# Two attention blocks on one core: a third tile for transposed blocks, and smaller work moved between the engines

## The chip, the core and the metric

The kernel runs on one core of a Trainium2 chip. The metric is the time of one execution on the device, in microseconds, as the median of several runs. The profile is of one further execution, taken by the hardware profiler; its rows carry the line numbers of the kernel before.

In what follows PE is the TensorE, DVE the VectorE, ACT the ScalarE and POOL the GpSimd engine; SP is the engine that here only issues transfers. Each engine works through its own instructions in order.

## The reference

Four images of 32 x 32 positions and 768 channels go through two attention layers. Each layer adds its result to its input:

```python
x = x + _L0_conv_ref(_gn(x), ...)      # 32 groups, no affine part
x = x + _L1_conv_ref(_gn(x), ...)
# in a layer, for each of 12 heads of 64 channels, S = 1024 positions:
q, k, v = ...                          # qkv = x @ Wqkv (second layer: + bias)
rel_h = jnp.einsum('bhwc,hkc->bhwk', r_q, Rh)
rel_w = jnp.einsum('bhwc,wkc->bhwk', r_q, Rw)
bias = rel_h[..., :, None] + rel_w[..., None, :]
attn = jax.nn.softmax(scale * q @ k.T + bias, axis=-1)
out = (attn @ v) @ Wproj + bproj
```

The second layer scales q once more before the position terms. Everything is float32.

## The kernel before

The two layers of four images make eight "images" in a row (`im` 0 to 7). The twelve heads of an image make six pairs (`pair` 0 to 5), so there are 48 pairs `g` in all. A pair has eight units `n`, each of 128 query positions for both heads. The main loop runs over (g, n); it writes out the order of every engine by hand (`tc.manual_schedule`), and overlaps the units like this. In the step of unit n the program emits

- what was queued for this step in the lists `early` and `later` (things put into `later` run two steps on, into `early` one step on),
- `biases` (L434, POOL) for unit n + 2, which forms the position bias of 128 x 1024 from the rows in `rel`,
- `scores` for unit n + 1: eight matmuls (L448), the addition of the bias with a running minimum (L457, DVE) and the exponential with its sum (L461, ACT),
- the reads back of transposed blocks, from the lists `behind` and `behind2` (L496, SP),
- `turn` for unit n (L485, DVE): 32 x 32 transposes into a tile `tb`; after every second unit, a quarter, the tile of each head is written to device memory (`td`, L488, SP) and later read back turned (`pt`),
- `divide` for unit n + 1: the reciprocal (L468, DVE) and the division of both heads' rows (L471, POOL),
- a share of the next pair's projections and of an output projection (`take(todo, share)`, PE), with their sums on DVE (L238, L240, L378, L379, L599, L601),
- after unit 6, `weigh` for quarters 0 and 1 (L514, PE, reads `pt` and v), and in unit 2 of the next pair for quarters 2 and 3.

Step 0 of the loop thus holds the scores of unit 1. Tiles come from pools; a tile whose pool has no free buffer makes its first writer wait for the last reader of the buffer's earlier tenant. `tb` has two buffers, one for each head. PSUM gives two tiles to scores (`ps_s`) and two to everything else (`ps_m`).

Position terms: `positions` multiplies q by a table (L396, PE), copies the result to a tile `t` (L401, ACT) and writes it to device memory (`tdr`, L403, issued by ACT). `diagonals` then reads it back along diagonals as `rel`, 16 transfers for each pair (L422, SP). They are issued in unit 4, ahead of quarter 1's `pt`.

Queries and keys: except in a plain pair (pair 0, and pair 1 of image 0) the projections use sums of inputs and of weights. `sum_weights` combines the weights of pair g + 2 in units 6 and 7 of pair g (L316 on ACT, L319, L321, L322 on DVE, L320, L323, L324 on POOL). `sum_input` combines the next image's columns in pair 5, one column in each of units 0 to 5 (L333 on ACT, L334 to L341 on DVE) and six halves in units 6 and 7 (L345).

Image boundary: in pair 4 the next image is loaded (L112), then normalised by `apply` in units 6 and 7 (L223, POOL except in image 0). Its statistics are gathered before. In images 0 to 2, columns of the next image pass through a tile `tmp` for that purpose, in units 5 and 7 of pairs 0 to 2.

Output: `project_out` (L590) reads the attention tiles and an output weight `wo`; the residual `res`, a tile of half an image row, is fetched ahead by `fetch` (L549, L569, SP), added to (L599, L601) and stored (L606). A `fetch` for the coming parts is queued in `later` behind each second part.

## Time and profile before

| what | value |
|---|---|
| median of three runs | 4094.45 us (4075.72, 4094.45, 4100.07) |
| the profiled execution | 4075.33 us, span of its instructions 4073.3 us |
| mean granted clock of PE | 0.947 |
| busy PE, DVE, POOL, ACT | 3568.1, 2951.5, 2893.8, 1177.7 us |
| moved by the DMA engines | 1089.25 MB, mean 267 GB/s |
| issues of td, pt, rel | 384, 384, 768 |

How to read its rows. A row of the windows view has the window, its length, then the busy time of PE, PE's weight loads (PEld), DVE, ACT and POOL, each with the number of instructions, and last the granted clock, the DMA engines' busy share and GB/s. A row of a timeline has the start and length in us, the engine, the line, the operation, the tile written and the tiles read, and the number of instructions merged; in brackets stands the idle time of the engine before it and what ended that. "SPq" is SP's queue of issues: its length is the time of issuing, not of the transfer. The trace counts two PE matmuls for each one that the program names (3072 for the 1536 of L448).

### The profile page before, as it was taken

Reading aid. Unit: us, or ns where it says so; the run is one execution under the profiler, and the core shown is the slowest. Engines: PE = TensorE matmul, PEld = TensorE weight load, DVE = VectorE, ACT = ScalarE, POOL = GpSimd, SP = SyncE. Lnnn points to the kernel's source line nnn. Section 1 sums busy time; section 2 is a strip of 40 time slices with the busy share of each in tenths; the row PEclk is TensorE's granted clock in tenths of the full one; section 3 lists DMA queues with packets and bytes.
Section 4 is the critical chain, followed back from the end, with each engine's and each line's share of the span. In section 5 each row is a group of like instructions: output and inputs, shape, how many; then the busy total and the mean of one; then the engine's idle time right before and its main releaser. Section 6 shows DMA issues by size and latency. Waiting matters only on the chain.

```text
span 4073.3 us, 55032 instructions
## 1 busy us (share of the span) xinstructions
PE 3568.1 (88%) x20652; PEld 1936.1 (48%) x20652; DVE 2951.5 (72%) x4197; ACT 1177.7 (29%) x1918; POOL 2893.8 (71%) x1771
## 2 busy tenths in 40 slices
PE   6989789897898978999789897899978999789999
PEld 3555355453454534545345453544535455344554
DVE  5967687776877768777687776867767677677776
ACT  2323232232232323323232232322323233222331
POOL 3877776777666777776776777777777776777774
PEclk9999899998999989999899998999989999899999
DMA  4778678786687876878678786788867788678878
GB/s 135 253 282 289 239 255 285 286 301 247 242 281 281 294 250 245 281 282 289 236 260 278 279 305 237 242 298 285 305 227 251 281 291 289 225 262 284 293 255 295
DMA packets 635659, 1089.25 MB, mean 267 GB/s; under 512 B 248320, under 2 KB 311296, under 8 KB 586240
## 3 DMA queue, kind: packets, MB, share of 16 engines
q1 hardware_dynamic: 579808, 1033.01, 71.8%
q10 hardware_dynamic: 55584, 52.72, 3.8%
q8 instruction: 162, 2.65, 0.3%
q14 instruction: 105, 0.86, 0.1%
HBM read 585.31 MB, written 500.27 MB: 267 GB/s over the span
## 4 chain that ended last, share of the span: by engine, by line
PE 51%; DVE 19%; DMA 16%; POOL 7%; issue 4%; SPq 2%; ACT 0%; DVEq 0%; ACTq 0%
PE pj L262 17%; DMA td<-tb 12%; PE av L514 11%; PE s L448 10%; PE o L590 6%; PE pv L364 5%; DVE tb L485 5%; POOL x L223 4%; DVE sc L457 3%; DMA pt<-td 2%; PE tp L396 2%; SPq L422 2%; DVE x L334 2%; POOL sc L434 1%; DVE x L345 1%
## 5 line engine op out<-in xcount | busy, mean ns | idle before, releaser
L471 POOL TENSOR_SCALAR sc<-sc,sm 128x1024 f32<-128x1024 f32 x768 | 916.2, 1204 | 1083.3 <-DVE sm L468 1076.5
L434 POOL TENSOR_TENSOR sc<-rel 128x1024 f32<-128x1024 f32 x768 | 1563.5, 2105 | 37.5 <-DMA rel<-tdr 37.5
L461 ACT ACTIVATE sc<-sc,sm 128x1024 f32<-128x1024 f32 x768 | 879.4, 1146 | 2274.0 <-DVE sm L457 2273.5
L485 DVE STREAM_TRANSPOSE tb<-sc 128x1024 f32<-128x1024 f32 x768 | 917.8, 1225 | 381.3 <-DMA td<-tb 378.0
L457 DVE CUSTOM_DVE_ANT_0 sc<-s,sc 128x1024 f32<-128x1024 f32 x768 | 909.6, 1221 | 263.8 <-PE s L448 177.3
L262 PE MATMUL pj<-x,w 64*128 64x512 f32 x4140 | 950.8, 601 | 81.0 <-POOL x L223 44.3
L514 PE MATMUL av<-pt,v 128*64 128x256 f32 x6144 | 763.7, 401 | 195.8 <-DMA pt<-td 110.6
L448 PE MATMUL s<-k,q 64*128 64x512 f32 x3072 | 767.4, 604 | 32.1 <-DVE sm L457 32.0
L590 PE MATMUL o<-attn,wo 128*128 128x512 f32 x1080 | 555.2, 668 | 189.4 <-DVE res L599 103.0
L514 PEld LDWEIGHTS av<-pt,v 128*64 128x64 f32 x6144 | 463.8, 144 | 525.5 <-DMA pt<-td 134.8
L262 PEld LDWEIGHTS pj<-x,w 64*128 64x128 f32 x4140 | 410.4, 190 | 589.6 <-issue 450.6
L364 PE MATMUL pv<-wv,x 64*128 64x256 f32 x4608 | 515.1, 376 | 0.4 <-DVE k L238 0.4
L364 PEld LDWEIGHTS pv<-wv,x 64*128 64x128 f32 x4608 | 448.0, 187 | 91.6 <-issue 40.9
L448 PEld LDWEIGHTS s<-k,q 64*128 64x128 f32 x3072 | 295.6, 190 | 349.9 <-issue 278.0
L590 PEld LDWEIGHTS o<-attn,wo 128*128 128x128 f32 x1080 | 218.1, 210 | 510.3 <-issue 271.2
L401 ACT COPY t<-tp 128x1024 f32<-128x1024 f32 x96 | 97.1, 1011 | 306.8 <-PE tp L396 265.1
L223 POOL TENSOR_SCALAR x<-x,nrm 128x512 f32<-128x512 f32 x84 | 176.6, 2115 | 0.0
L238 DVE TENSOR_TENSOR k<-pj,k 128x512 f32<-128x512 f32 x173 | 117.7, 689 | 63.0 <-PE pj L262 46.3
L461 ACT ACTIVATION_READ_ACCUMULATOR sc<-sc,sm 128x1 f32 x768 | 143.2, 186 | 0.0
L599 DVE SCALAR_TENSOR_TENSOR res<-o,bo,res 128x512 f32<-128x512 f32 x88 | 64.4, 745 | 91.0 <-PE o L590 90.7
L396 PEld LDWEIGHTS tp<-tab,q 64*128 64x128 f32 x1536 | 98.0, 188 | 45.1 <-issue 42.4
L601 DVE TENSOR_TENSOR res<-o,res 128x512 f32<-128x512 f32 x92 | 62.0, 683 | 70.1 <-PE o L590 69.4
(57 smaller groups left out, 1607.9 us busy)
## 6 DMA issues: line engine op xcount, KB each, us to landing
td<-tb SPq DMA_DIRECT2D x384, 1024.0 KB, 6.0
pt<-td SPq DMA_DIRECT2D x382, 1024.0 KB, 7.6
tdr<-t ACTq DMA_DIRECT2D x96, 512.0 KB, 6.6
w<-in_wqk SPq DMA_DIRECT2D x96, 384.0 KB, 6.6
rel<-tdr SPq DMA_DIRECT2D x760, 32.0 KB, 2.2
x<-in_x SPq DMA_DIRECT2D x84, 256.0 KB, 6.4
part<-res SPq DMA_DIRECT2D x84, 256.0 KB, 3.1
res<-part SPq DMA_DIRECT2D x84, 256.0 KB, 8.4
```

Of the source, the lines that this page charges most:

```text
L223: (nc.gpsimd if im else nc.vector).tensor_scalar(x, x, nrm[:, c, 0:1], nrm[:, c, 1:2], ALU.subtract, ALU.mult)
L262: nc.tensor.matmul(t[:, a, :], lhsT=w[rows, c, :], rhs=x[c][rows, :], start=(c == 0), stop=(c == len(x) - 1),)
L364: nc.tensor.matmul(t[:, a, k, :], lhsT=xs[i // 2 * NC + c][rows, at * P : (at + 1) * P], rhs=w[rows, c, :], start=(c == 0), stop=(c == NC ...
L396: nc.tensor.matmul(ps[:, h, j, :], lhsT=q[rows, at * P : (at + 1) * P], rhs=tabs[l][rows, :], start=True, stop=True,)
L434: nc.gpsimd.tensor_tensor(sc.rearrange("p (a k) (u l) -> p a l (k u)", a=4, l=8), rel[:, h, 0, n, :].unsqueeze(1).unsqueeze(2).to_broadcas ...
L448: nc.tensor.matmul(ps[h][:, cols], lhsT=q[rows, n * P : (n + 1) * P], rhs=k[rows, cols], start=True, stop=True,)
L457: nc.vector.tensor_tensor_reduce(out=sc, in0=ps[h], in1=sc, scale=-scale, scalar=BIG, op0=ALU.add, op1=ALU.min, accum_out=st[:, 0, h : h + 1],
L461: nc.scalar.activation(sc, sc, AF.Exp, bias=st[:, 0, h : h + 1], scale=-1.0, accum_out=st[:, 1, h : h + 1],)
L471: nc.gpsimd.tensor_scalar(sc, sc, st[:, 2, h : h + 1], 1.0, ALU.mult, ALU.mult)
L485: nc.vector.transpose(tb[:, :, j, :], sc_of[g, n, h])
L514: nc.tensor.matmul(av[rows, at * 2 * P : (at + 1) * 2 * P], lhsT=v_of[g][:, k, rows], rhs=pt_of[g, quarter, h][:, :, k, :], start=(k == 0) ...
L590: nc.tensor.matmul(t, lhsT=wo_of[im, o, c], rhs=attn_of[im * NP + c][:, cols], start=(c == c0), stop=(c == c1 - 1),)
```

## The change

- The pool of transposed tiles `tb` gets three buffers.
- Bias rows: `rel` becomes two tiles of four units each, with three buffers in all; `diagonals` issues 32 transfers of 16 KB instead of 16 of 32 KB.
- The pool `tmp` goes. Position copies and the columns for the statistics use the `res` tiles (four buffers, half the size), so a position copy becomes two, each with its own transfer. The statistics' columns are loaded in unit 1 of every pair (image 0: units 1 and 4 of pairs 0 to 2).
- `fetch` for a pair's four output parts runs in unit 5.
- The attention tile of a pair becomes two halves, eleven buffers instead of six whole ones.
- The query sums read PSUM and write the query in order, and read the key tile in steps, where they wrote in steps.
- Weights: the first sum moves from DVE to POOL; the two sums into `w4` become ACT copies of POOL's difference.
- Divisions: head 0 on POOL, head 1 on ACT.
- `apply` runs on DVE, spread over units 2, 4, 6 and 7.
- `sum_input` is spread over four steps for a column: ACT copy, POOL difference, DVE sum (with an ACT copy for the first three), DVE difference.

The core of the diff:

```diff
     xpool = ctx.enter_context(tc.tile_pool(name="x", bufs=1))
-    apool = ctx.enter_context(tc.tile_pool(name="attn", bufs=6))
+    apool = ctx.enter_context(tc.tile_pool(name="attn", bufs=11))
     qkpool = ctx.enter_context(tc.tile_pool(name="qk", bufs=2))
...
     scpool = ctx.enter_context(tc.tile_pool(name="sc", bufs=6))
-    tmppool = ctx.enter_context(tc.tile_pool(name="tmp", bufs=1))
-    tbpool = ctx.enter_context(tc.tile_pool(name="tb", bufs=2))
+    tbpool = ctx.enter_context(tc.tile_pool(name="tb", bufs=3))
     ptpool = ctx.enter_context(tc.tile_pool(name="pt", bufs=2))
-    relpool = ctx.enter_context(tc.tile_pool(name="rel", bufs=2))
+    relpool = ctx.enter_context(tc.tile_pool(name="rel", bufs=3))
     iopool = ctx.enter_context(tc.tile_pool(name="io", bufs=4))
...
         x, y = x_of[im - 1], y_of[im - 1]
-        x_of[im] = y[NC:] + x[:NC] + y[:3]
+        x_of[im] = spare(im - 1) + y[:3]
         y_of[im] = y[3:NC] + x[NC:]
+    def spare(im):
+        return y_of[im][NC:] + x_of[im][:NC]
     def load_x(im, c, i, to=None):
...
             x = x_of[im][i * NC + c]
-            (nc.gpsimd if im else nc.vector).tensor_scalar(
+            nc.vector.tensor_scalar(
                 x, x, nrm[:, c, 0:1], nrm[:, c, 1:2], ALU.subtract, ALU.mult
...
-        by = lambda x: x.rearrange("p (m a) -> p a m", a=4)
-        t = [by(t[:, a, :]) for a in range(2)]
-        q = [by(qk_of[g, 0][:, i * HALF : (i + 1) * HALF]) for i in range(2)]
+        q = [
+            qk_of[g, 0][:, i * HALF : (i + 1) * HALF].rearrange("p (m a) -> p m a", a=4)
+            for i in range(2)
+        ]
         k = qk_of[g, 1].rearrange("p (a m) -> p a m", a=4)
         k = [k[:, :, i * P : (i + 1) * P] for i in range(2)]
+        u = [t[:, a, :].rearrange("p (m a) -> p m a", a=4) for a in range(2)]
+        t = [x.rearrange("p m a -> p a m") for x in u]
         bias = [None, None]
...
             nc.scalar.copy(k[0], t[0])
-            add(q[0], t[1], k[0], bias[0])
+            add(q[0], u[1], k[0].rearrange("p a m -> p m a"), bias[0])
         elif unit == 1:
...
             add(k[1], t[0], k[0])
-            add(q[1], t[1], k[1], bias[0])
+            add(q[1], u[1], k[1].rearrange("p a m -> p m a"), bias[0])
         else:
...
         def second():
-            nc.vector.tensor_tensor(w3[TOP], w3[TOP], w[1][TOP], ALU.add)
+            nc.gpsimd.tensor_tensor(w3[TOP], w3[TOP], w[1][TOP], ALU.add)
             nc.gpsimd.tensor_tensor(w3[LOW], w3[TOP], w[0][TOP], ALU.subtract)
-            nc.vector.tensor_tensor(w4[TOP], w3[TOP, :3], w[0][TOP, :3], ALU.subtract)
-            nc.vector.tensor_tensor(w4[LOW], w3[TOP, 3:], w[0][TOP, 3:], ALU.subtract)
+            nc.scalar.copy(w4[TOP], w3[LOW, :3])
+            nc.scalar.copy(w4[LOW], w3[LOW, 3:])
             nc.gpsimd.tensor_tensor(w3[LOW], w[0][LOW], w3[LOW], ALU.subtract)
...
         xs, ys = x_of[im], y_of[im]
-        if n < NC:
-            a, b, y, z = xs[n], xs[NC + n], ys[n], ys[NC + n % 3]
+        def of(c):
+            return (xs[c], xs[NC + c], ys[c], ys[NC + c % 3]) if 0 <= c < NC else 4 * [None]
+        a, b, y, z = of(n)
+        if a is not None:
             nc.scalar.copy(y[LOW], b[TOP])
-            nc.vector.tensor_tensor(y[TOP], b[LOW], y[LOW], ALU.subtract)
-            if n < 3:
-                nc.vector.tensor_tensor(z[TOP], y[TOP], a[TOP], ALU.add)
-                nc.vector.tensor_tensor(y[LOW], y[TOP], a[TOP], ALU.add)
-                nc.vector.tensor_tensor(y[LOW], y[LOW], a[LOW], ALU.subtract)
-            else:
-                nc.vector.tensor_tensor(z[LOW], y[TOP], a[TOP], ALU.add)
-                nc.vector.tensor_tensor(y[LOW], z[LOW], a[LOW], ALU.subtract)
-            return
-        for c in range(3 * (n - NC), 3 * (n - NC) + 3):
-            a, b = xs[c], xs[NC + c]
-            (nc.gpsimd if c < 3 else nc.vector).tensor_tensor(b[TOP], b[TOP], a[TOP], ALU.subtract)
+        a, b, y, z = of(n - 1)
+        if a is not None:
+            nc.gpsimd.tensor_tensor(y[TOP], b[LOW], y[LOW], ALU.subtract)
+        a, b, y, z = of(n - 2)
+        if a is not None:
+            half = TOP if n - 2 < 3 else LOW
+            nc.vector.tensor_tensor(z[half], y[TOP], a[TOP], ALU.add)
+            if n - 2 < 3:
+                nc.scalar.copy(y[LOW], z[TOP])
+        a, b, y, z = of(n - 3)
+        if a is not None:
+            nc.vector.tensor_tensor(y[LOW], (y if n - 3 < 3 else z)[LOW], a[LOW], ALU.subtract)
+        for c in range(3 * n - 18, 3 * n - 15) if n in (6, 7) else ():
+            a, b, y, z = of(c)
+            (nc.gpsimd if c in (0, 3, 4) else nc.vector).tensor_tensor(
+                b[TOP], b[TOP], a[TOP], ALU.subtract
+            )
...
                 )
-        t = tmppool.tile([P, 4, 2, P], FP, tag="tmp", name=f"t_{g}_{i}")
-        nc.scalar.copy(t, ps.rearrange("p h j r -> p j h r"))
         td = t_of[g]
-        nc.scalar.dma_start(
-            out=td[i * HALF : (i + 1) * HALF, :].rearrange("(j p) r -> p j r", p=P),
-            in_=t.rearrange("p j h r -> p j (h r)"),
-        )
+        for k in range(2):
+            if g + 1 < NPAIR:
+                t = iopool.tile([P, 2, 2, P], FP, tag="res", name=f"t_{g}_{i}_{k}")
+            else:
+                t = spare(g // NP)[4 + 2 * i + k].rearrange("p (j h r) -> p j h r", j=2, h=2)
+            nc.scalar.copy(t, ps[:, :, 2 * k : 2 * k + 2, :].rearrange("p h j r -> p j h r"))
+            at = (2 * i + k) * 2 * P
+            nc.scalar.dma_start(
+                out=td[at : at + 2 * P, :].rearrange("(j p) r -> p j r", p=P),
+                in_=t.rearrange("p j h r -> p j (h r)"),
+            )
         if i == 1:
...
         td = t_of[g]
-        for h in range(2):
-            for ax in range(2):
-                for y in range(4):
+        rel_of[g] = []
+        for half in range(2):
+            rel = relpool.tile([P, 2, 2, NT // 2, HW], FP, tag="rel", name=f"rel_{g}_{half}")
+            rel_of[g].append(rel)
+            for h in range(2):
+                for ax in range(2):
+                    for y in range(4):
-                    at = HW * y * 2 * P + h * P + HW - 1 + 2 * HW * ax - (y if ax == 0 else 0)
-                    src = bass.AP(
-                        td.tensor, td.offset + at,
-                        [[2 * P - ax, HW], [P * 2 * P - (4 if ax == 0 else 0), NT], [1, HW]],
-                    )
-                    (nc.scalar if h and not g else nc.sync).dma_start(out=rel_of[g][32 * y : 32 * y + 32, h, ax, :, :], in_=src)
+                        step = P * 2 * P - (4 if ax == 0 else 0)
+                        at = HW * y * 2 * P + h * P + HW - 1 + 2 * HW * ax - (y if ax == 0 else 0)
+                        src = bass.AP(
+                            td.tensor, td.offset + at + half * (NT // 2) * step,
+                            [[2 * P - ax, HW], [step, NT // 2], [1, HW]],
+                        )
+                        (nc.scalar if h and not g else nc.sync).dma_start(
+                            out=rel[32 * y : 32 * y + 32, h, ax, :, :], in_=src
+                        )
...
             sc = sc_of[g, n, h].rearrange("p k j -> p (k j)")
-            nc.gpsimd.tensor_scalar(sc, sc, st[:, 2, h : h + 1], 1.0, ALU.mult, ALU.mult)
+            if h == 0:
+                nc.gpsimd.tensor_scalar(sc, sc, st[:, 2, h : h + 1], 1.0, ALU.mult, ALU.mult)
+            else:
+                nc.scalar.activation(sc, sc, AF.Copy, scale=st[:, 2, h : h + 1])
...
-        if quarters[0] == 0:
-            attn_of[g] = apool.tile([P, S], FP, tag="attn", name=f"attn_{g}")
+        half, first = divmod(quarters[0], 2)
+        if first == 0:
+            attn_of[g, half] = apool.tile([P, HALF], FP, tag="attn", name=f"attn_{g}_{half}")
         n = len(quarters)
...
             nc.tensor.matmul(
-                t, lhsT=wo_of[im, o, c], rhs=attn_of[im * NP + c][:, cols],
+                t, lhsT=wo_of[im, o, c], rhs=attn_of[im * NP + c, i],
                 start=(c == c0), stop=(c == c1 - 1),
...
                 fetch(place[im, p, o, i] + 4)
-            else:
-                later.append(lambda: fetch(place[im, p, o, i] + 4))
         yield True
...
         run(later)
-        fetch(3)
         biases(0, 0)
...
             early, later = later, early
-            if im + 1 < B and pair < 3 and n in (5, 7):
-                c = 2 * pair + n // 7
-                passing = tmppool.tile([P, S], FP, tag="tmp", name=f"x_{im + 1}_{c}")
+            upto = 4 * (pair % 3) + 3
+            if n == 5 and (im, pair) >= (0, 3):
+                fetch(place[((im, 0) if pair >= 3 else (im - 1, 1)) + divmod(upto, 2)])
+            ask = [divmod(g + 3, NP)] if n == 1 else []
+            if im == 0 and pair < 3:
+                ask = [(0, 2 * pair + n // 4)] if n in (1, 4) else []
+            for im2, c in ask if im < B else ():
                 for i in range(2):
-                    x = passing[:, i * HALF : (i + 1) * HALF]
-                    load_x(im + 1, c, i, x)
-                    later.append(lambda c=c, i=i, x=x: stats(im + 1, c, i, x))
+                    if im2 + 1 < B:
+                        x = iopool.tile([P, HALF], FP, tag="res", name=f"x_{im2 + 1}_{c}_{i}")
+                        load_x(im2 + 1, c, i, x)
+                        later.append(lambda im=im2 + 1, c=c, i=i, x=x: stats(im, c, i, x))
             if at + 2 < len(units):
...
                 divide(*units[at + 1])
-            if pair == 4 and n in (6, 7) and not end:
-                for c in range(4) if n == 6 else range(4, NX):
+            if pair == 4 and not end:
+                for c in {2: (0, 1), 4: (2, 3), 6: (4, 5, 6), 7: range(7, NX)}.get(n, ()):
                     apply(c % NC, c // NC)
...
                 sum_input(im + 1, n)
-            elif g == 0:
-                sum_input(0, n)
+            elif g == 0 or pair == 0 and n == 0:
+                sum_input(im, n if g == 0 else NT)
+            elif g == 1 and n == 0:
+                sum_input(0, NT)
             take(todo, share)
```

`spare(im)` names the nine input tiles that are free after the image's pair 4 (`y_of[im][NC:] + x_of[im][:NC]`). The places where a tile's new half is indexed, in `biases`, in the rest of `weigh`, and where `spare` takes the place of the same expression, are left out.

More of the change, by code (lines that the diff above doesn't have):

```diff
@@ L279, in project_in @@
             if which == 0:
-                to = qk_of[g, 0][:, i * HALF : (i + 1) * HALF].rearrange("p (m a) -> p m a", a=4)
-                t = [x.rearrange("p a m -> p m a") for x in t]
+                to, t = q[i], u
             if images[im][0] == 0:
@@ L389, in positions @@
             t_of[g] = dram2.tile([S, 2 * P], FP, tag="tdr", name=f"tdr_{g}")
-            rel_of[g] = relpool.tile([P, 2, 2, NT, HW], FP, tag="rel", name=f"rel_{g}")
         ps = ps_m.tile([P, 2, 4, P], FP, tag="m", name=f"tp_{g}_{i}")
@@ L411, in diagonals @@
         td = t_of[g]
-        for h in range(2):
-            for ax in range(2):
-                for y in range(4):
-                    at = HW * y * 2 * P + h * P + HW - 1 + 2 * HW * ax - (y if ax == 0 else 0)
-                    src = bass.AP(
-                        td.tensor, td.offset + at,
-                        [[2 * P - ax, HW], [P * 2 * P - (4 if ax == 0 else 0), NT], [1, HW]],
-                    )
-                    (nc.scalar if h and not g else nc.sync).dma_start(out=rel_of[g][32 * y : 32 * y + 32, h, ax, :, :], in_=src)
+        rel_of[g] = []
[14 more added lines that the diff above has]
+                        )
     sc_of, st_of, tb_of, pt_of, attn_of = {}, {}, {}, {}, {}
     def biases(g, n):
-        rel = rel_of[g]
+        rel, m = rel_of[g][n // 4], n % 4
         for h in range(2):
@@ L435, in biases @@
                 sc.rearrange("p (a k) (u l) -> p a l (k u)", a=4, l=8),
-                rel[:, h, 0, n, :].unsqueeze(1).unsqueeze(2).to_broadcast(shape),
-                rel[:, h, 1, n, :].rearrange("p (l a) -> p a l", a=4).unsqueeze(3).to_broadcast(shape),
+                rel[:, h, 0, m, :].unsqueeze(1).unsqueeze(2).to_broadcast(shape),
+                rel[:, h, 1, m, :].rearrange("p (l a) -> p a l", a=4).unsqueeze(3).to_broadcast(shape),
                 ALU.add,
@@ L517, in weigh @@
                     )
-        at = quarters[0] * 2 * P
-        to = attn_of[g][:, at : at + n * 2 * P].rearrange("p (q n r i) -> p q r n i", q=n, n=2, r=4)
+        at = first * 2 * P
+        to = attn_of[g, half][:, at : at + n * 2 * P].rearrange("p (q n r i) -> p q r n i", q=n, n=2, r=4)
         av = av.rearrange("p (q r n i) -> p q r n i", q=n, n=2, r=4)
@@ L565, in fetch @@
             else:
-                res = (y_of[im][NC:] + x_of[im][:NC])[2 * o + i - 4]
+                res = spare(im)[2 * o + i - 4]
             res_of[im, p, o, i] = res
```

## The prediction

> **What bounds the kernel now.** I read the page's totals and chain first, then the stretch of each pair of heads, then SP's and DVE's timelines in an ordinary pair.
>
> ```profile
> PE 3568.1 (88%) x20652; PEld 1936.1 (48%) x20652; DVE 2951.5 (72%) x4197; ACT 1177.7 (29%) x1918; POOL 2893.8 (71%) x1771
> ...
> PE pj L262 17%; DMA td<-tb 12%; PE av L514 11%; PE s L448 10%; PE o L590 6%; PE pv L364 5%; DVE tb L485 5%; POOL x L223 4%; DVE sc L457 3%; DMA pt<-td 2%; PE tp L396 2%; SPq L422 2%; DVE x L334 2%; POOL sc L434 1%; DVE x L345 1%
> ```
>
> TensorE carries half the chain; the rest is the trip of the transposed blocks through memory (td), some DVE, and POOL's normalisation (L223). Two rows of the windows view, a boundary pair (pair 5) and an ordinary one:
>
> ```profile
> 2477.90:2577.50 99.60, 79.59 (x441) 41.37 (x441) 77.43 (x94) 29.85 (x49) 79.90 (x45) 0.91 0.63 222
> 2662.70:2740.70 78.00, 71.99 (x427) 39.69 (x426) 54.01 (x81) 23.98 (x40) 56.52 (x36) 0.96 0.82 289
> ```
>
> The boundary pair is 21.6 us longer, with POOL busy 79.9 us. To see where, I cut each pair into eight stretches, from the start of L457 of one unit to that of the next, averaged over images 1 to 6. Pairs 0 to 5 take 87.5, 79.2, 79.6, 77.8, 82.9, 98.7 us. In pairs 1 to 4, stretches 1 to 6 (about 48 us) have PE busy throughout; the idle time lies in stretch 0 (17.3, 17.3, 16.8, 16.5 us, PE busy some 13) and stretch 7 (14.3, 14.5, 12.8, 16.4). Where no weights are combined before it, in pair 5, stretch 0 takes 12.4 us with PE full. In pair 5 stretches 1 and 2 take 22.0 and 16.7 us instead of some 7 and 8: POOL runs twelve L223 of 2.1 us there, and PE waits for x. Pair 0 opens with 26.1 us.
>
> SP's timeline in the ordinary pair 25, from unit 3 on, then PE's and DVE's:
>
> ```profile
> 2210.28 1.46 SPq L488 DMA_DIRECT2D td<-tb  x2
> 2212.14 9.91 SPq L422 DMA_DIRECT2D rel<-tdr  x16
> 2222.17 1.66 SPq L126 DMA_DIRECT2D w<-in_wqk  x1
> 2223.87 0.99 SPq L496 DMA_DIRECT2D pt<-td  x2
> 2224.95 1.31 SPq L488 DMA_DIRECT2D td<-tb  x2
> ```
>
> ```profile
> 2227.17 4.10 PE L514 MATMUL av<-pt,v 128*64 128x256 f32 x34
> 2233.33 3.67 PE L514 MATMUL av<-pt,v 128*64 128x256 f32 x30 [2.06 <-DMA pt<-td]
> ...
> 2250.87 5.26 PE L590 MATMUL o<-attn,wo 128*128 128x512 f32 x6 [4.04 <-DVE res L601]
> ```
>
> ```profile
> 2235.88 1.25 DVE L485 STREAM_TRANSPOSE tb<-sc 128x1024 f32<-128x1024 f32 x1 [6.13 <-DMA td<-tb]
> 2238.47 1.25 DVE L485 STREAM_TRANSPOSE tb<-sc 128x1024 f32<-128x1024 f32 x1 [1.35 <-DMA td<-tb]
> ...
> 2246.39 0.92 DVE L319 TENSOR_TENSOR w<-w,w 64x768 f32<-64x768 f32 x1
> 2247.35 1.35 DVE L321 TENSOR_TENSOR w<-w,w 64x384 f32<-64x384 f32 x1
> 2248.72 1.38 DVE L322 TENSOR_TENSOR w<-w,w 64x384 f32<-64x384 f32 x1
> 2250.12 0.69 DVE L601 TENSOR_TENSOR res<-o,res 128x512 f32<-128x512 f32 x1
> ```
>
> SP issues without a pause from 2210 to 2226. The block that PE wants in unit 6 (pt, quarter 1) is asked for at 2223.87, right behind sixteen rel transfers; both halves are there at 2233.3, and PE has waited 2.06 us. That is stretch 7. Then three weight sums hold L601, which PE needs: 4.04 us idle, and the next six matmuls take 5.26 us (877 each, against 444 in the group of 18 before): the clock fell. That is stretch 0.
>
> **The change, part by part.**
>
> *Bias rows in half tiles.* `diagonals` issues 32 transfers of 16 KB for 16 of 32 KB, all on SP ahead of quarter 1's pt. The price of one issue is the open number. Thirteen rel issues from 2215.62 take 6.43 us, 0.495 each; ten x loads of 256 KB at the start take 4.65 us, 0.465 each. Eight times the bytes costs no more, so I take the issue as fixed: 16 x 0.495 = 7.9 us more per pair. The bounds are 0 (price follows size) and 7.9; rel issues with a gap before them take 0.30, which would make 32 x 0.345 less 16 x 0.495, 3.1. Nothing covers it: PE already waits for this pt. Its later half lands on average 5.8 us after the start of stretch 7 (pairs 0 to 3), 8.3 in pair 4. In pair 4, where PE waits longest and restarts at half clock, stretch 7 is that landing plus 8.1 us. So after: 5.8 + 7.9 + 8.1 = 21.8 us in pairs 0 to 3, 24.3 in pair 4.
>
> [...]
>
> *Three tb tiles.* Two heads share the tag. With three, unit 6's first transpose (6.13 us wait here) goes at once, but the second takes the tile whose td was issued first, still in flight. It now waits for the first landing (2235.8), not the second (2238.4): 2.6 us earlier if nothing moved. But `fetch` moves to unit 5, six issues (6 x 0.48 = 2.9 us) and 1.4 MB ahead of td; at the 2.4 us that a megabyte takes between td's two landings that is 3.3 us more. The first td lands 8.5 us into stretch 7 now, 8.5 + 7.9 + 3.3 = 19.7 after, and L457 follows 2.1 us later: 21.8, the same as by PE. So the third tile gains nothing while the burst is paid.
>
> *Weights combined on GpSimd.* L319, L321, L322 (1.26 + 1.51 + 1.38 us mean) leave DVE; POOL gets a fourth sum of 2.0 us, ACT two copies of some 0.5. L601 goes 3.65 us earlier, the idle time and the half clock go, and stretch 0 falls to pair 5's 12.4: 4.9 + 4.9 + 4.4 + 4.1 = 18.3 us per image. POOL has room (16 us busy in stretch 0, 6.5 in stretch 1); w4 is needed only after 5 us of the next projection.
>
> *Normalisation on DVE, spread.* Twelve of 2.11 us leave POOL, the 25 us of pair 5. On DVE the row of image 0 is 0.55 us; the sums of SBUF tiles there, beside a busy POOL, take 1.06 to 2.21 us, so 0.55 to 2.2, and I take 0.8. Three stand behind unit 6's transposes (stretch 7 of pair 4 to 25.5), five ahead of L599 in unit 7 (stretch 0 of pair 5 to 16).
>
> [...] No row of before shows L223 on DVE beside POOL.
>
> *Input sums.* DVE keeps five operations for every two columns where it had eight; POOL takes one of 1.3 us per column. Pair 5 becomes 16 + 7.2 + 8 + 10 + 26.7 (stretches 4 to 6) + 20 (stretch 7: td, then four such sums) = 88 us, 10.7 less. Pair 0 opens with 17 us instead of 26.1, 9.1 less.
>
> *Beside other work.* 384 divisions go from POOL (1.20 us) to ACT (1.15 as Exp; ACT is 29% busy). Position copies: four of 0.6 us for two of 1.0, two more ACT issues of 0.37; both under PE's full stretches. The copies now share the ring of four "res" tiles with results and statistics' loads, ten tiles a pair: a copy in unit 2 waits for a result stored two units before (part lands in 3.1 us), so nothing; if ACT were late there, diagonals would be late next. The statistics' loads of images 0 to 2 pass from units 5 and 7 to unit 1 on SP, ahead of a td that DVE fills later in that unit: nothing. Half attention tiles only free space. Query sums (L238, L240: 1.11, 1.17 us) trade a strided write for a strided read: 0.69 to 1.76 by the contiguous row and the slowest sum of that width; I take no change, under PE in stretches 1 to 3, where DVE has 1 to 4 us free.
>
> *Sum per middle image:* pairs 1 to 3 in stretch 7, 3 x 21.8 - 41.6 = +23.8; pair 0, 21.8 - 13.6 = +8.2; pair 4, +9.1; sums -18.3; pair 5 -10.7; pair 0's start -9.1. Together +3.0, six times 18. Image 0 has no output work in two of its stretches 0, +19; image 7 has no boundary, +20. So +57 on the profiled execution's 4075.33 (span 4073.3): 4132, a ratio of 1.014; on the median 4094.45 that is 4150.
>
> **Rivals.** *The issue is cheaper than back-to-back rows say* (0.345, so 3.1 us): 4.8 us less in 39 pairs, 185 us: 3965, not slower. For it: spaced issues of 0.30. Against: 0.465 for another shape. It decides below about 6.5 us per pair. *The burst costs nothing*: stretch 7 stays near 14, 7.8 x 40 = 315 less: 3835. *DVE becomes the bound around the boundary*: normalisation and sums, locked out by POOL, cost 1.5 us more each over twelve normalisations, 18 us in seven boundaries, 126: 4275. For it the 1.76 and 2.21 us rows; against, POOL is idle more. *The change doesn't do what it says* holds in part already: the third tile frees one head of two.
>
> **How the numbers follow.** A measurement here tells about 1%. Forecast 0.48 (4070 to 4230 by itself), cheaper issue 0.28, free burst 0.07, DVE bound 0.13, else 0.04. Of the forecast, 0.02 falls on faster, 0.10 on same, 0.36 on slower; of the cheaper issue 0.26 and 0.02; the rest as they stand, else half same, half slower: faster 0.35, same 0.14, slower 0.51. The range leaves out the free burst and the far ends: 3890 to 4280.
>
> **What would show it.** Right: SP's rel burst some 18 us long; PE's wait for pt in unit 6 near 9 us in pairs 0 to 4; a wait of the second transpose only; stretch 0 near 12.4 us; pair 5 below 90. Wrong: rel issues under 0.4 us, or PE's wait for pt still near 2 us.

## The result, and the profile after

The changed kernel takes 4193.0 us (median of four runs, 4176.2 to 4205.3) where the kernel before takes 4085.4 (median of four). The ratio is 1.026, with a 95% interval of 1.0205 to 1.031: slower. The profiled execution took 4205.27 us, its span is 4203.3 us, the mean granted clock 0.926 (0.947 before).

The page of the changed kernel: busy time of each engine, then the chain of work that ended last, by engine and by line. (L445 is rel's issue, L482 the scores' pass on DVE, L513 the transposes, L516 td, L524 pt, L543 the product with v, L226 the normalisation, L354 and L357 input sums, L628 and L630 the results.)

```profile
PE 3588.6 (85%) x20652; PEld 1950.1 (46%) x20652; DVE 2791.9 (66%) x4092; ACT 1678.8 (40%) x2500; POOL 2379.7 (57%) x1390
...
PE 41%; DMA 17%; DVE 16%; SPq 13%; issue 6%; POOL 5%; ACT 2%; ACTq 0%; DVEq 0%; POOLq 0%
PE pj L265 13%; SPq L445 12%; PE o L619 9%; DMA pt<-td 9%; PE s L473 8%; PE av L543 7%; DVE tb L513 6%; DMA td<-tb 6%; DVE sc L482 4%; POOL sc L459 3%; PE pv L378 2%; DVE x L354 2%; DVE x L226 1%; PE tp L409 1%; DVE x L357 1%
```

DVE lost 160 us of work and POOL 514, and both only have more idle time. What is new in the chain is SP: 12% of the span runs through the issues of rel (L445), where L422 held 2% before. The normalisation, 4% on POOL before (L223), is now 1% on DVE (L226); the input sums hold 3% as they did before (L354 and L357, then L334 and L345).

The waits of the changed kernel (engine and line, what it waited for, us in total, times, the longest):

```profile
DVE tb L513 <- DMA td<-tb: 666.0, 49, 20.0
PE av L543 <- DMA pt<-td: 380.5, 91, 11.0
```

The same ordinary pair as in the prediction, pair 25, on SP, DVE and PE:

```profile
2263.88 18.40 SPq L445 DMA_DIRECT2D rel<-tdr  x32
2282.39 0.36 SPq L129 DMA_DIRECT2D w<-in_wqk  x1
2282.80 0.98 SPq L524 DMA_DIRECT2D pt<-td  x2
2283.83 1.25 SPq L578 DMA_DIRECT2D wo<-in_wo  x2
2285.17 2.07 SPq L598 DMA_DIRECT2D res<-part  x4
2289.17 3.12 SPq L516 DMA_DIRECT2D td<-tb  x2
```

```profile
2282.92 1.24 DVE L513 STREAM_TRANSPOSE tb<-sc 128x1024 f32<-128x1024 f32 x1
2299.47 1.25 DVE L513 STREAM_TRANSPOSE tb<-sc 128x1024 f32<-128x1024 f32 x1 [15.31 <-DMA td<-tb]
```

```profile
2279.22 3.67 PE L543 MATMUL av<-pt,v 128*64 128x256 f32 x32
2289.15 1.11 PE L543 MATMUL av<-pt,v 128*64 128x256 f32 x2 [6.26 <-DMA pt<-td]
2291.96 6.48 PE L543 MATMUL av<-pt,v 128*64 128x256 f32 x30 [1.69 <-DMA pt<-td]
```

The burst of 32 issues takes 18.40 us where 16 took 9.91. Quarter 1's pt is asked for behind it, and PE waits 7.95 us for its two halves, against 2.06 before. The first transpose of unit 6 goes at once (the third tile), the second waits 15.31 us for td. That td's tile was full when the transposes of unit 5 ended at 2277.9; it was issued at 2289.17.

The stretches of a pair, cut as in the prediction (from the start of L457, now L482, of one unit to that of the next), averages over images 1 to 6, us:

| stretch | pair 0 | pair 1 | pair 2 | pair 3 | pair 4 | pair 5 |
|---|---|---|---|---|---|---|
| 0, before | 26.1 | 17.3 | 17.3 | 16.8 | 16.5 | 12.4 |
| 0, after | 16.6 | 12.0 | 11.8 | 11.9 | 12.1 | 19.5 |
| 1, before | 9.4 | 9.8 | 9.8 | 9.8 | 9.4 | 22.0 |
| 1, after | 13.5 | 9.4 | 9.4 | 9.4 | 9.5 | 7.9 |
| 7, before | 13.6 | 14.3 | 14.5 | 12.8 | 16.4 | 5.7 |
| 7, after | 21.5 | 19.8 | 21.3 | 19.4 | 28.2 | 24.5 |
| all eight, before | 87.5 | 79.2 | 79.6 | 77.8 | 82.9 | 98.7 |
| all eight, after | 90.2 | 80.7 | 80.9 | 81.2 | 88.9 | 96.9 |

An image goes from 505.7 to 518.8 us: what stretch 0 gives, stretch 7 takes, and more.

### The profile page after: what moved, and what is told of

Read it like the earlier page. It is cut to its first block, busy times and chain, and to the rows that moved or that the text cites. A ratio compares the mean times of both kernels' runs of the same rounds, so it can differ in the third digit from the quotient of the medians.

```text
span 4203.3 us, 56667 instructions
## 1 busy us (share of the span) xinstructions
PE 3588.6 (85%) x20652; PEld 1950.1 (46%) x20652; DVE 2791.9 (66%) x4092; ACT 1678.8 (40%) x2500; POOL 2379.7 (57%) x1390
## 4 chain that ended last, share of the span: by engine, by line
PE 41%; DMA 17%; DVE 16%; SPq 13%; issue 6%; POOL 5%; ACT 2%; ACTq 0%; DVEq 0%; POOLq 0%
PE pj L265 13%; SPq L445 12%; PE o L619 9%; DMA pt<-td 9%; PE s L473 8%; PE av L543 7%; DVE tb L513 6%; DMA td<-tb 6%; DVE sc L482 4%; POOL sc L459 3%; PE pv L378 2%; DVE x L354 2%; DVE x L226 1%; PE tp L409 1%; DVE x L357 1%
## 5 line engine op out<-in xcount | busy, mean ns | idle before, releaser
L459 POOL TENSOR_TENSOR sc<-rel 128x1024 f32<-128x1024 f32 x768 | 1547.8, 2085 | 38.5 <-DMA rel<-tdr 35.2
L497 POOL TENSOR_SCALAR sc<-sc,sm 128x1024 f32<-128x1024 f32 x384 | 455.1, 1185 | 1672.1 <-DVE sm L493 1656.1
L513 DVE STREAM_TRANSPOSE tb<-sc 128x1024 f32<-128x1024 f32 x768 | 914.1, 1223 | 666.1 <-DMA td<-tb 666.0
L486 ACT ACTIVATE sc<-sc,sm 128x1024 f32<-128x1024 f32 x768 | 880.2, 1147 | 988.0 <-DVE sm L482 959.3
L543 PE MATMUL av<-pt,v 128*64 128x256 f32 x6144 | 843.5, 424 | 389.5 <-DMA pt<-td 380.5
L482 DVE CUSTOM_DVE_ANT_0 sc<-s,sc 128x1024 f32<-128x1024 f32 x768 | 908.1, 1220 | 179.2 <-PE s L473 115.4
L265 PE MATMUL pj<-x,w 64*128 64x512 f32 x4140 | 939.1, 599 | 60.3 <-DVE x L226 26.6
L499 ACT ACTIVATE sc<-sc,sm 128x1024 f32<-128x1024 f32 x384 | 441.0, 1148 | 1111.9 <-DVE sm L493 1111.9
L543 PEld LDWEIGHTS av<-pt,v 128*64 128x64 f32 x6144 | 485.9, 153 | 776.8 <-DMA pt<-td 437.1
L473 PE MATMUL s<-k,q 64*128 64x512 f32 x3072 | 749.3, 599 | 14.5 <-DVE sm L482 12.5
L619 PE MATMUL o<-attn,wo 128*128 128x512 f32 x1080 | 526.2, 641 | 143.6 <-DVE res L628 62.6
L473 PEld LDWEIGHTS s<-k,q 64*128 64x128 f32 x3072 | 288.3, 188 | 311.3 <-issue 280.2
L419 ACT COPY t<-tp 128x512 f32<-128x512 f32 x188 | 110.0, 585 | 140.5 <-PE tp L409 89.7
L393 DVE TENSOR_TENSOR v<-pv,v 128x256 f32<-128x256 f32 x192 | 81.5, 425 | 79.9 <-ACT v L390 76.5
L628 DVE SCALAR_TENSOR_TENSOR res<-o,bo,res 128x512 f32<-128x512 f32 x88 | 64.2, 741 | 79.0 <-PE o L619 79.0
```

What stands on the lines that cost most here:

```text
L265: nc.tensor.matmul(t[:, a, :], lhsT=w[rows, c, :], rhs=x[c][rows, :], start=(c == 0), stop=(c == len(x) - 1),)
L459: nc.gpsimd.tensor_tensor(sc.rearrange("p (a k) (u l) -> p a l (k u)", a=4, l=8), rel[:, h, 0, m, :].unsqueeze(1).unsqueeze(2).to_broadcas ...
L473: nc.tensor.matmul(ps[h][:, cols], lhsT=q[rows, n * P : (n + 1) * P], rhs=k[rows, cols], start=True, stop=True,)
L482: nc.vector.tensor_tensor_reduce(out=sc, in0=ps[h], in1=sc, scale=-scale, scalar=BIG, op0=ALU.add, op1=ALU.min, accum_out=st[:, 0, h : h + 1],
L486: nc.scalar.activation(sc, sc, AF.Exp, bias=st[:, 0, h : h + 1], scale=-1.0, accum_out=st[:, 1, h : h + 1],)
L497: nc.gpsimd.tensor_scalar(sc, sc, st[:, 2, h : h + 1], 1.0, ALU.mult, ALU.mult)
```

## The experiments

The theory: sixteen more issues on SP, at some 0.5 us each whatever their size, delay pt and td by 8 us in each pair and eat a large gain from the weights. The rival: the loss is in the other parts (the third tile, the earlier fetch, the work handed to DVE).

**Half of the burst one stretch later (e1).** In the changed kernel:

```diff
-            later.append(lambda: diagonals(g))
+            later.append(lambda: diagonals(g, (0,) if g else (0, 1)))
...
             run(behind)
             behind, behind2 = behind2, behind
+            if n == 0 and g:
+                diagonals(g, (1,))
```

> The changed kernel, with the second half of the bias rows (16 of the 32 transfers) issued one stretch later, in unit 0 of the pair that uses them, so that 16 instead of 32 issues stand ahead of quarter 1's pt and td. Theory (each of the 16 added issues costs SP some 0.5 us, and pt, then td, come that much later): the burst falls from 18.5 to some 10 us, stretch 7 of pairs 0 to 4 from 19 to 28 us to some 14 to 20, 6 to 8 us for each of 40 pairs: 3870 to 3990 us, 200 to 320 below the changed kernel. Rival (the stretch is long for another reason, the three transposed-block tiles or the earlier fetch): 4150 or more, stretch 7 still near 20 us.

Measured 3892.5 us, 0.9525 of before (0.9505 to 0.9546), 300 less than the changed kernel. Stretch 7 of pairs 0 to 4 is 13.8, 13.1, 14.7, 13.4, 18.2 us. The issues and the bytes are the same and only their place is another: the theory holds.

**And the fetch back in unit 6 (e2).**

```diff
-            if n == 5 and (im, pair) >= (0, 3):
+            if n == 6 and (im, pair) >= (0, 3):
```

> The run before it, and in it the fetch of the next pair's weights is back in unit 6, behind the td issues of unit 5, where the kernel before has it. Theory: td's landing, and by it the second transpose of unit 6, comes another 3 us earlier where the landing of td sets the end, so 0 to 3 us for each of some 38 pairs: 0 to 115 us below the run before it. Rival (pt, not td, sets the end of stretch 7): no difference over 1%.

Measured 3835 us, 0.939 (0.9368 to 0.9412). Stretch 7 falls to 11.7, 11.6, 12.0, 12.4, 14.6 us. In e1 td ended it: in pairs 0 to 3 the first td landed 11.1 to 12.7 us into the stretch and the second transpose followed at once. Here it lands 3.4 to 4.2 us earlier, but the stretch shortens by only 1.0 to 2.7, since now PE's work behind pt ends it: in these pairs PE is done with the next unit's scores 0.1 to 0.2 us before the stretch is over.

**The kernel before with its transfers split (e3).**

```diff
-                    (nc.scalar if h and not g else nc.sync).dma_start(out=rel_of[g][32 * y : 32 * y + 32, h, ax, :, :], in_=src)
+                    for half in range(2):
+                        src = ...   # units 4 * half to 4 * half + 3
+                        (...).dma_start(out=rel_of[g][32 * y : 32 * y + 32, h, ax, 4 * half : 4 * half + 4, :], in_=src)
```

> The kernel before, with one edit: each of the 16 bias-row transfers of 32 KB is issued as two of 16 KB into the same tile. Same bytes, same tiles, same place. Theory (price per issue): the burst grows from 10 to some 18 us, pt of quarter 1 lands 7.9 us later in each of 40 pairs: 4290 to 4415 us, 200 to 330 above the kernel before. Rival (the price follows the size, or the second half of the transfers hides): within 1% of 4085 us.

Measured 4464 us, 1.0935 of before (1.0914 to 1.0957): this one edit costs 378 us, more than the whole change. SP in pair 25 of this kernel:

```profile
2416.23 18.48 SPq L424 DMA_DIRECT2D rel<-tdr  x32
2434.82 0.36 SPq L126 DMA_DIRECT2D w<-in_wqk  x1
2435.23 0.98 SPq L501 DMA_DIRECT2D pt<-td  x2
2436.31 0.93 SPq L493 DMA_DIRECT2D td<-tb  x2
```

The same bytes in twice the issues take 18.48 us, 0.58 each. Stretch 7 of pairs 0 to 3 is 21.6, 21.7, 22.1, 20.9 us. The total lies above the range because pairs 5 and 0, which had been left out of the count, pay as well: 6.5 us in stretch 7 of pair 5, 5.2 in stretch 0 of pair 0.

**The changed kernel with whole transfers (e4), and with two block tiles (e5).** Whole tiles need more room, so e4 also goes back to two tb buffers; e5 makes that step alone.

```diff
-    tbpool = ctx.enter_context(tc.tile_pool(name="tb", bufs=3))
+    tbpool = ctx.enter_context(tc.tile_pool(name="tb", bufs=2))   # e4 and e5
-    relpool = ctx.enter_context(tc.tile_pool(name="rel", bufs=3))
+    relpool = ctx.enter_context(tc.tile_pool(name="rel", bufs=2)) # e4: whole tiles, 16 issues
```

> The changed kernel with whole bias-row tiles (two of them, 16 transfers of 32 KB), and two instead of three tiles for transposed blocks to make room for them; all else as changed. Theory (the halving alone makes stretch 7 long, and the third block tile gives 2 to 3 us for a pair at most): burst some 10 us, stretch 7 near 14 to 17 us, 3890 to 4000 us. Rival (the moved fetch and the work handed to DVE make stretch 7 long): 4150 us or more. Rival (the third tile is what holds the time down): above 4200 us.

> The changed kernel with two tiles for transposed blocks instead of three. Theory (with the long burst, td's landing ends stretch 7, and the third tile lets unit 6's second transpose start at the first landing of td, not at the second, 2.4 us earlier): 2.4 us more for each of 40 pairs, 4260 to 4310 us. Rival (quarter 1's pt ends the stretch, and the third tile frees nothing): within 1% of the changed kernel's 4193 us.

Measured: e4 3948 us, 0.9668 (0.9652 to 0.9684), with stretch 7 of pairs 0 to 3 at 16.7, 15.6, 16.4, 14.1 us; e5 4286 us, 1.0492 (1.0473 to 1.051). Between them lies only the halving of the bias rows: 338 us. Between e5 and the changed kernel lies only the third tile: it is worth 93 us. SP in pair 25 of e4:

```profile
2123.49 11.25 SPq L441 DMA_DIRECT2D rel<-tdr  x16
2134.85 0.38 SPq L129 DMA_DIRECT2D w<-in_wqk  x1
2135.28 0.98 SPq L518 DMA_DIRECT2D pt<-td  x2
```

**The weights alone (e6).** In the kernel before, the three DVE sums of the weights become one POOL sum and two ACT copies, as in the change.

```diff
-            nc.vector.tensor_tensor(w3[TOP], w3[TOP], w[1][TOP], ALU.add)
+            nc.gpsimd.tensor_tensor(w3[TOP], w3[TOP], w[1][TOP], ALU.add)
...
-            nc.vector.tensor_tensor(w4[TOP], w3[TOP, :3], w[0][TOP, :3], ALU.subtract)
-            nc.vector.tensor_tensor(w4[LOW], w3[TOP, 3:], w[0][TOP, 3:], ALU.subtract)
+            nc.scalar.copy(w4[TOP], w3[LOW, :3])
+            nc.scalar.copy(w4[LOW], w3[LOW, 3:])
```

> The kernel before, with one part of the change: the weights are combined on GpSimd and ACT. Theory (the sums on DVE held the first result in stretch 0, and its clock fell): stretch 0 of pairs 1 to 4 from some 17 to 12.4 us, 18 us for each of 7 images, 3945 to 3975 us. Rival (the time comes back in the waits of stretch 7, or GpSimd holds up the bias sums): 4040 us or more.

Measured 3856 us, 0.9444 (0.9418 to 0.9471), a gain of 229 us, nearly twice the expected one. Stretch 0 of pairs 1 to 4 falls to 11.3, 11.5, 11.7, 11.1 us, below the 12.4 of pair 5 that served as a model, and that of pair 0 from 26.1 to 18.3. The other stretches stay. So the gain is real, and the changed kernel has it (its stretch 0 is as short); the halving takes it away.

**The normalisation on ACT (e7), then the last sums on POOL (e8).** Both in the kernel of e2. e7 makes the mean term a bias, so that ACT normalises in one instruction:

```diff
+            nc.vector.scalar_tensor_tensor(mv[:, 0, 0:1], mv[:, 0, 0:1], -1.0, mv[:, 2, 0:1], ALU.mult, ALU.mult)
...
-            nc.vector.tensor_scalar(x, x, nrm[:, c, 0:1], nrm[:, c, 1:2], ALU.subtract, ALU.mult)
+            nc.scalar.activation(x, x, AF.Identity, bias=nrm[:, c, 0:1], scale=nrm[:, c, 1:2])
```

e8 adds:

```diff
-            nc.vector.tensor_tensor(y[LOW], (y if n - 3 < 3 else z)[LOW], a[LOW], ALU.subtract)
+            (nc.gpsimd if n - 3 == 5 else nc.vector).tensor_tensor(
+                y[LOW], (y if n - 3 < 3 else z)[LOW], a[LOW], ALU.subtract
+            )
...
-            (nc.gpsimd if c in (0, 3, 4) else nc.vector).tensor_tensor(
+            nc.gpsimd.tensor_tensor(
```

The first is L354, the second L357. What led to these edits is a reading of the changed kernel at the end of pair 4: DVE, POOL and PE.

```profile
2548.32 2.25 DVE L226 TENSOR_SCALAR x<-x,nrm 128x512 f32<-128x512 f32 x1
...
2556.55 6.56 DVE L226 TENSOR_SCALAR x<-x,nrm 128x512 f32<-128x512 f32 x5
2563.03 1.40 DVE L628 SCALAR_TENSOR_TENSOR res<-o,bo,res 128x512 f32<-128x512 f32 x2
```

```profile
2556.72 1.33 POOL L497 TENSOR_SCALAR sc<-sc,sm 128x1024 f32<-128x1024 f32 x1 [4.25 <-DVE sm L493]
2558.02 4.36 POOL L459 TENSOR_TENSOR sc<-rel 128x1024 f32<-128x1024 f32 x2
```

```profile
2563.83 4.57 PE L619 MATMUL o<-attn,wo 128*128 128x512 f32 x6 [6.63 <-DVE res L628]
```

The five take 0.52, 1.34, 2.24, 2.24 and 0.53 us: the first has begun before POOL does, the next three end 0.28 us after the end of a POOL instruction (L497, then each L459), the last runs when POOL is done. L628 stands behind them, and PE waits 6.63 us for it. The sums do worse. One of them in image 3, beside POOL:

```profile
1632.22 6.33 DVE L354 TENSOR_TENSOR x<-x,x 64x512 f32<-64x512 f32 x1
```

```profile
1629.14 4.01 POOL L459 TENSOR_TENSOR sc<-rel 128x1024 f32<-128x1024 f32 x2
1633.03 1.12 POOL L497 TENSOR_SCALAR sc<-sc,sm 128x1024 f32<-128x1024 f32 x1
1634.11 3.95 POOL L459 TENSOR_TENSOR sc<-rel 128x1024 f32<-128x1024 f32 x2
```

It starts at 1632.22 and ends 0.49 us after the last of these, four POOL instructions later. In 40 of its 48 the same sum takes 1.50 us, and those too end 0.54 us after the end of a POOL instruction, but of the first one. How long it takes with POOL idle isn't shown; the sum L349, of the same shape and begun before POOL's instruction in all its 48, takes 0.67.

> The faster of the runs so far (half of the bias rows one stretch later, fetch in unit 6), with the normalisation as scale and bias on ACT instead of DVE, in the same places. Theory (DVE's normalisations wait for GpSimd's instructions, 2.24 us beside the bias sums and 0.53 alone; the five in unit 7 hold L628 and PE for 6.6 us): stretch 0 of pair 5 from 19.5 to some 13.5 us, stretch 7 of pair 4 some 2.5 us shorter, 8.5 us for each of 7 boundaries, 3760 to 3790 us. Rival (PE waits there for something else, or ACT's exponentials come as late): 3815 us or more.

> The run before it, and in it the sums of the next input that DVE did in units 6 and 7 (L357) and the last column's difference (L354) go to GpSimd. Theory (these DVE sums take 5.5 to 6.3 us where GpSimd runs instructions back to back, 1.5 us otherwise, and hold what PE waits for at the start of pair 0): stretch 0 and 1 of pair 0 from 16.5 and 13.6 to some 13.5 and 9.5 us, stretch 7 of pair 5 some 2 us shorter, 9 us for each of 7 boundaries, 3700 to 3730 us. Rival (GpSimd's bias sums come later and hold the scores instead): no gain, 3760 us or more.

Measured: e7 3781 us, 0.926 (0.9238 to 0.9281); e8 3708 us, 0.9077 (0.9062 to 0.9093). The rows of the groups in e8 (busy us, mean ns; L229 is the normalisation, L355 what was L354):

```profile
L229 ACT ACTIVATE x<-x,nrm 128x512 f32<-128x512 f32 x96 | 70.5, 799 | 4.3 <-DMA nrm<-back 4.3
L355 DVE TENSOR_TENSOR x<-x,x 64x512 f32<-64x512 f32 x40 | 60.7, 1518 | 1.2
...
L355 POOL TENSOR_TENSOR x<-x,x 64x512 f32<-64x512 f32 x8 | 10.2, 1275 | 0.7
```

In e7 stretch 0 of pair 5 goes from 19.5 to 12.4 us, as expected; stretch 7 of pair 4 goes the other way, 14.6 to 18.2. That is a wait which moved: stretches 3 to 5 of this pair are 3.6 us shorter, the burst of rel ends at the same time of the pair as before (63 us after its start), and the whole pair takes 82.2 us against 81.8. In e8 stretch 1 of pair 0 goes from 13.5 to 9.4 and stretch 7 of pair 5 from 15.1 to 8.1; stretch 0 of pair 0, expected to fall to 13.5, stays at 17.2. Both totals fell into their ranges, but not by the stretches named alone: stretch 7 of pair 5 gave 7 us where e8 expected 2, and stretch 7 of pair 4 in e7 and stretch 0 of pair 0 in e8 gave none of what was expected of them.

**The fetch alone (e9).** The changed kernel with e2's one line:

> The changed kernel with one edit: the fetch of the next weights is back in unit 6. The prediction on record held that pt and td end stretch 7 at the same time (21.8 us by either), so that this alone gains nothing: within 1% of 4193 us. Theory from the trace of the changed kernel (td of unit 5 is ready at 2277.9, is issued only at 2289.2 behind the fetch, when the first pt has landed, and its landing alone ends the stretch): td goes some 5 us earlier, pt then sets the end, 2 to 3 us less for each of some 38 pairs, 4080 to 4120 us.

Measured 4168 us, 1.0204 of before (1.0172 to 1.0237), 25 us below the changed kernel. Stretch 7 of pairs 0 to 3 stays at 21.5, 20.6, 21.5, 18.9 us; only pairs 4 and 5 give 3 us each. PE and DVE in pair 25 of e9 (L473 are the scores, L482 the pass on DVE that begins the next stretch):

```profile
2266.52 1.11 PE L543 MATMUL av<-pt,v 128*64 128x256 f32 x2 [6.77 <-DMA pt<-td]
2270.07 5.70 PE L543 MATMUL av<-pt,v 128*64 128x256 f32 x30 [2.44 <-DMA pt<-td]
2275.71 1.99 PE L473 MATMUL s<-k,q 64*128 64x512 f32 x8
```

```profile
2272.59 1.25 DVE L513 STREAM_TRANSPOSE tb<-sc 128x1024 f32<-128x1024 f32 x1 [11.57 <-DMA td<-tb]
2277.84 1.22 DVE L482 CUSTOM_DVE_ANT_0 sc<-s,sc 128x1024 f32<-128x1024 f32 x1 [1.14 <-PE s L473]
```

The second transpose goes at 2272.59, but the next stretch begins only at 2277.84, when the scores behind pt are there. While the burst is long, pt ends the stretch as well as td does; the theory drawn from one pair's td was too simple, and the recorded prediction was right here.

**A quarter of the burst elsewhere (e10, e11).** In e8, the eight issues of the second head of the first half go behind unit 5's td (e10), or right behind quarter 1's pt (e11):

```diff
-            later.append(lambda: diagonals(g, (0,) if g else (0, 1)))
+            if g:             # now diagonals(pair, half, heads)
+                later.append(lambda: diagonals(g, 0, (0,)))
+                rest.append(lambda: diagonals(g, 0, (1,)))
...
+            if n == 4:        # e11, behind run(behind); in e10: n == 5, behind turn(g, n)
+                run(rest)
```

> The fastest run so far, and in it the second head's eight issues of the first half of the bias rows go behind the td of unit 5, so that eight instead of sixteen stand ahead of quarter 1's pt and td. Theory (what is left of idle time in stretch 7 is still the burst): pt and td 4 us earlier, stretch 7 of pairs 0 to 3 from some 12 to 10 us, of pair 4 from 18.4 to some 14, 12 us for each of 8 images, 3600 to 3640 us. Rival (the bias sums of the next pair's unit 0 now wait for their rows and hold the scores): no gain or a loss, 3700 us or more.

> As e10, but the second head's eight issues stand directly behind quarter 1's pt and ahead of the td of unit 5, so that only pt is helped. Theory (e10's gain in stretch 7 was lost to bias rows that landed after unit 0's bias sums wanted them and to wo behind them; issued ahead of td they come in time): stretch 7 of pairs 0 to 3 some 1 to 2 us shorter than in e8, stretch 0 near 12.4 to 13, 3640 to 3690 us. Rival (td, which is not helped, ends stretch 7 in most pairs): within 1% of 3708 us.

e10 takes 3709 us, 0.9082 (0.9046 to 0.9118), no gain. Stretch 7 fell as expected, to 9.0, 8.0, 9.0, 6.9 us, and stretch 0 gave it back (13.0, 16.2, 14.2, 16.2 in pairs 1 to 4). SP, POOL and PE of e10 show how (L454 is rel, L525 td, L468 the bias sums, L587 wo, L628 the output product):

```profile
2010.84 1.46 SPq L525 DMA_DIRECT2D td<-tb  x2
2012.35 12.09 SPq L454 DMA_DIRECT2D rel<-tdr  x8
2024.49 0.91 SPq L587 DMA_DIRECT2D wo<-in_wo  x2
```

```profile
2025.87 2.04 POOL L468 TENSOR_TENSOR sc<-rel 128x1024 f32<-128x1024 f32 x1 [10.62 <-DMA rel<-tdr]
```

```profile
2027.05 7.51 PE L628 MATMUL o<-attn,wo 128*128 128x512 f32 x13 [3.73 <-DMA wo<-in_wo]
```

Eight issues behind two td transfers of 1 MB take 12.09 us, and both the bias rows and wo behind them come late. With the issues ahead of td, e11 takes 3673 us, 0.8984 (0.8956 to 0.9011), the fastest kernel here, PE busy for 94% of the span:

```profile
PE 3443.7 (94%) x20652; PEld 1926.1 (52%) x20652; DVE 2590.0 (71%) x3972; ACT 1743.9 (48%) x2596; POOL 2407.4 (66%) x1422
```

The total lies in its range, but the theory held in part only. The bias sums now wait 163 us in all for rel, against 459 in e10 and 46 in e8. PE still waits for wo, 89 us against 70 in e10 and 9 in e8, and stretch 0 is 14.1, 15.1, 14.6, 16.4 us where 12.4 to 13 was expected. The gain over e8 comes from stretch 7, which fell by more than the expected 1 to 2 us: 9.0, 8.3, 9.2, 7.9 us in pairs 0 to 3, 13.5 in pair 4.

## Why the prediction was right, and where it was not

The forecast case came out: slower, by the burst. Its sum gave +57 us on the profiled execution, where 130 were measured; +3.0 per middle image, where 13.1 were measured. Between the medians it is 108 us, and 4193 lies 43 above the forecast 4150. The mechanism was right, but the total came this near partly by luck. Per middle image, stretch 7 of pairs 1 to 3 was put 4.9 us too long and the gain in stretch 0 of pairs 1 to 4 1.8 too small; against that stand 8.9 us too little in pair 5, 4.1 in pair 0's stretch 1 and 2.7 in pair 4's stretch 7.

- **The price of an issue: right.** Taken as 0.495 us whatever the size, 7.9 us for sixteen more. The burst is 18.40 us, 8.5 more than before, 0.53 for each of the sixteen, and e3 puts the arithmetic to the test by itself: stretch 7 was to be 5.8 + 7.9 + 8.1 = 21.8 us and is 21.6, 21.7, 22.1, 20.9. "The burst costs nothing" and "the issue is cheaper" are out.
- **Where stretch 7 ends: right, but a wrong conclusion.** The prediction had td and pt both at 21.8 us, and e9 confirms that moving the fetch away gains little. In pairs 0 to 3 td lands 17.2 to 19.4 us into the stretch (19.7 expected), though the sum had left out that td's issue also waits for a landing of pt (see the last section). "So the third tile gains nothing while the burst is paid" does not follow from a tie: without it td is later than pt. e5 shows stretch 7 at 23.9, 22.7, 24.1, 21.9 us, 2.4 to 2.9 more, and 93 us in all.
- **Weights: the place right, the size too small.** Stretch 0 was to be 12.4 us in pairs 1 to 4 and is 11.8 to 12.1. But pair 0's start was put down to the input sums (-9.1 us; measured -9.5), and e6 shows that 7.8 us of it come from the weights alone: that number came out right for a wrong reason. The term was 18.3 us per image; in e6 the five pairs give 30.1.
- **Normalisation on DVE: mis-sized.** Taken at 0.8 us with bounds of 0.55 and 2.2; the mean is 1.145 us. Pair 5's stretch 0 was to be 16 us and is 19.5, which is the five instructions at 6.56 us instead of 4.0, and some idle time more; pair 4's stretch 7 was to be 25.5 and is 28.2.
- **Input sums: mis-sized, beyond the bounds.** Mean rows of 1.06 to 2.21 us were the price. Such a mean hides two cases: of the 48 sums of L334 (1.76 us in the mean) 41 took 0.69 us and six 8.9, beside a run of POOL instructions. In the changed kernel the means are 2.35 us (L354) and 3.14 us (L357). Pair 5's stretch 7 was to be 20 us and is 24.5; pair 0's stretch 1, which had no term, grew by 4.1. With the term before it this is the rival "DVE becomes the bound around the boundary" coming true in part: pair 5 was to take 88 us and takes 96.9.

What that rival calls "locked out by POOL" stands in the rows. Of the 96 normalisations 46 take 0.5 us and 50 end 0.28 us (0.278 to 0.283) after the end of a POOL instruction; in the kernel before, the six long sums of L334 end 0.47 to 0.48 us after the end of one. The rival's 1.5 us more for each normalisation, 18 us at a boundary, was the author's estimate and too high, since only half of them met POOL, and those waited 1.2 us in the mean: 96 x (1.145 - 0.53) = 59 us over seven boundaries, 8.4 each, and e7 won back 54 us in all.

What the parts are worth by themselves: weights -229 us (on the kernel before), halved bias rows +338 (with two tiles), third tile -93, earlier fetch +25. They add up to +41, where +108 was measured between the medians. The rest lies in the other parts of the change, and e6 and e4 bound it: e4 has the weights, whole bias rows, two block tiles and all the other parts, and is 92 us slower than e6, which has the weights alone. So the moved normalisation, input sums, divisions and copies and the earlier fetch together cost 92 us. The fetch is 25 of it by e9 and 58 by the step from e1 to e2, which leaves 34 to 67. By stretches, e4 loses 13.6 us against e6 in stretch 7 of pair 5 and 7.4 in its stretch 0, and wins 22.3 back in its stretches 1 and 2; what is left is mostly stretch 7 of pairs 0 to 4, 13.0 us per image. The rival was right that these parts cost time, but the halving costs far more.

## What to carry to other kernels

Count the transfers that a queue must issue ahead of the one that the bound waits for, not their bytes: here halving a tile to save memory doubled that count, and the same bytes took SP 18.40 us to issue instead of 9.91, 12% of the span on the chain that ended last. Before moving small work to an engine that looks idle, look at which engine runs beside it at that moment, and which result stands behind it in the queue: 6 us of normalisations ahead of one result cost PE 6.6 us. And where a part of a change gains much by itself (e6, 229 us), undoing the other parts one at a time shows more than the total does.

## What the runs showed of the hardware that was not expected

- A DVE sum with two inputs in SBUF can wait for several POOL instructions in a row. All 48 instructions of L354 end 0.48 to 0.54 us after the end of a POOL instruction: 40 after the first that ends (1.50 us in all), seven after the fourth (6.0 to 6.4), one after the sixth (9.1). What decides between them was not tried. It is not only a pause of POOL, since in eight of the 40 POOL's next instruction had begun, by its record, before the one waited for ended. The normalisation, with one input, nearly always gets in after the first that ends (48 of the 50).
- Part of SP's time is a wait that the rows of its issues don't name. In the changed kernel td, ready at 2277.9, was issued at 2289.17, when the first half of pt, the eighth transfer ahead of it, had landed (PE goes on at 2289.15). The view of SP's own waits has it as `SPq L516 <- DMA pt<-td: 159.0, 72, 3.5` (159.0 us in 72 times; 51.7 us in the kernel before). It is a limit of eight transfers under way, and the program sets it. All 3240 transfers that SP and ACT issue in the changed kernel tell of their landing by eight semaphores, and ahead of this td stands an SP instruction that waits for the one of that pt and ends at 2289.14. None of the 3232 transfers that take over a semaphore is issued before the transfer that had it has landed, and 211 go within 0.1 us of that. On SP, no transfer of the changed kernel (3018 that have an eighth ahead) or of the kernel before (2258) is issued before that eighth has landed. In e10 the eight issues behind td, from 2012.35 to 2024.44, last past the landing of pt, with which PE goes on at 2017.74, and that of a td, with which DVE goes on at 2020.27; which of them waited for which landing was not shown. Whether the chip would carry more than eight was not tried.
- Moving the three weight sums took PE's stretch 0 below the pair that never had them (11.1 to 11.7 against 12.4 us). Why was not tried.
